# A two-layer graph kernel: fences on TensorE's own queue, a half clip ahead of the logits, gathers behind folds, loads in halves, more logits inside the products

## The chip, the cores and the metric

The kernel runs on one core of one Trainium2 chip. The metric is the device time of one launch in microseconds (us). A core has TensorE (PE in the profile, with its weight loads as PEld), VectorE (DVE), ScalarE (ACT), GpSimd (POOL) and SyncE (SP, which here only issues DMAs and, before the change, empty instructions). Each has its own in-order queue; SP and POOL issue the DMAs, all of which share 16 DMA engines.

## The reference

Eight graphs of 2048 nodes with 256 features share one 0/1 adjacency. Layer 0 is attention in chunks: for every query the softmax is taken in each chunk of 256 keys by itself, and the eight results are added. Layer 1 is graph attention over all keys.

```python
# layer 0 (4 heads of 64, 8 chunks of 256 keys)
h = maximum(layernorm(x), 0); q, k, v = projections of h
scores = clip(q.k / 8, -10, 10);  scores = where(adj == 0, -10, scores)
attn = softmax(scores within each chunk);  ctx = sum over chunks of attn @ v
out = layernorm(ctx @ Wo.T + bo + h) * gamma + beta;  x = x + out
# layer 1
h = maximum(layernorm(x), 0) @ W
e = leaky_relu(h.a1 + (h.a2)^T);  e = where(adj == 0, -1e9, e)
x = x + maximum(softmax(e) @ h, 0)
```

## The kernel before

**Layer 0** is class `Attention`. One batch has 32 steps: 4 blocks of 512 queries times 8 chunks of 256 keys (two key tiles, `kt` 0 and 1). Everything is float32, and one head has 64 rows, so TensorE works on half its rows (64 of 128) and on a quarter of its columns (32) at a time: a "slot" is four such column tiles of 512 queries, in the two passes that float32 takes here. A step has 17 slots, named by two digits in `slots` (L680): eight `o` (logits of heads 0 to 3 and key tile 0 or 1, L555, into the PSUM tile `ps_s`, one tile with both key tiles of a head), eight `v` (values, L570: half 0 or 1 and turn 0 or 1 in the first digit, key tile in the second, into `ps_n`), and one `s` (sums of the exponentials, L592, into `ps_t`). A slot uses the low or the high half of the rows; two neighbours on different halves run side by side, so the order in `begin` (L695) and `end` (L724) is written as pairs. There are two `ps_s`, two `ps_n` and two `ps_t`.

The logits of step `f` pass through DVE (`clip`, L604: the clip and the adjacency in one instruction, both key tiles at once, or in two "half clips" for head 0 of the next step at the end of an even step), ACT (`exponentials`, L616), POOL (`add`, L623, two key tiles added, two instructions a step), a DMA that adds the upper half of the rows to the lower (`fold`, L630, from POOL's queue), TensorE's sums two steps later, ACT (`invert`, L636), DVE (`scale`, L649: `ps_n` times the inverse, into `prod`, two instructions) and a second accumulating DMA (`gather`, L653: `prod` is added to `ctxT` in SBUF; POOL's queue as well). `prod` has two buffers, and all gathers of one block of queries add to one tile, so that each waits for the one before it to land. Before the change `gather(f - 3)` is issued in `end(f)` between the two adds, after whatever `begin(f)` and `end(f)` run "beside" the step on POOL.

The values of turn 0 and turn 1 of one half write the same bank of PSUM from different halves of the rows. `fence` (L522) keeps them apart: an empty instruction on SP waits for the turn-0 matmuls, and the turn-1 matmuls wait for it. SP issues in order all of the kernel's other loads: the adjacency bounds (L179), the transposed features (L163, whose issue waits for the sends of L151), `x` and `h` of a block (L787, L798). `output_tiled` (L811), the output projection, uses the same fence.

**Beside the attention**, class `Between` (L774) does the rest of layer 0 and the start of layer 1 for the block that is ready: its table `beside` (L965) gives a half step (`begin` or `end`) to every piece: loads, features, output projection (L806, L828), layer norms, the value matmuls of layer 1. `adjacency` (L329) does the finds and turns of the adjacency matrix in batch 0, and the table `once` the weights of layer 1 (`layer1_vector`, L1220).

**Layer 1** is `weights` (L1063, DVE, ACT and POOL make the exponentials), `products` (L1083; 64 matmuls of 128x128 by 128x257 for each of 16 pieces, L1090) and `finish` (L1103). The loop over `pieces1` also prepares the projection of the batch after next (`far`), and calls `Attention.early` in its last pieces, which places logits, clips and exponentials of the next batch's first step into the products.

The accumulators of layer 1 are two `ps_s` halves or `ps_n`/`ps_t`; the tile that `add` and `fold` write is the one that layer 1 used as `g`, so that the first add of a batch waits for the last product of the batch before it (releaser "PE ps_t L1090").

Of the kernel before, what the change touches and what calls it, by code (L numbers as in the profile page):

```python
# [17 lines left out]
P = 128  # L18
# [13 lines left out]
def gnn_two_layers(  # L32
# [296 lines left out]
    def adjacency(parts):  # L329
# [14 lines left out]
        finds = [9, 10, 13, 14, 17, 18, 21, 22]  # L344
        turns = [12, 14, 16, 18, 20, 22, 24, 30]
# [176 lines left out]
    def fence(before, after):  # L522

        nop = nc.sync.nop()
        for x in before:
            tc.add_manual_dep(nop.ins, x.ins.name, SYNC, reason="both write one bank of PSUM")
        for x in after:
            tc.add_manual_dep(x.ins, nop.ins.name, SYNC, reason="both write one bank of PSUM")


    class Attention:
# [28 lines left out]
        def values(self, n, half, turn, kt):  # L560
# [4 lines left out]
            if (n, c) not in self.num:  # L565
                self.num[n, c] = ps_n()
            made = []
# [9 lines left out]
            elif kt == 0:  # L577
                fence(self.before.pop((n, c)), made)
# [79 lines left out]
        def early(self, part):  # L658
# [16 lines left out]
            if part == 3:  # L675
                for kt in range(KT):
                    self.logits(1, 0, kt)
                    self.logits(1, 1, kt)

        def slots(self, f, *names):  # L680


            for name in names:
                kind, what, kt = name[0], int(name[1]), int(name[2])
                if kind in "oc":
                    n = f + (what < 2) + (kind == "c")
                    if self.has(n) and (n > 1 or n == 1 and what > 1):
                        self.logits(n, what, kt)
# [6 lines left out]
        def begin(self, f, pieces=()):  # L695
# [10 lines left out]
            if f == 1:  # L706
                self.clip(1, 0)
                self.exponentials(1, 0)
            self.clip(f, 1)
            self.clip(f, 2)  # L710
            self.exponentials(f, 1)
            self.exponentials(f, 2)
            if f == 1:
                self.add(0, 0)
                self.add(0, 1)
                self.fold(0)
            if self.has(f) and odd:
# [6 lines left out]
        def end(self, f, pieces=()):  # L724
# [6 lines left out]
            else:  # L731
                self.slots(f, "v20", "s00", "v21", "o01")
            self.clip(f, 3)
            self.run(pieces, None)
            if odd:
                self.clip(f + 1, 0)
            else:
                self.clip(f + 1, 0, slice(0, 1))
                self.clip(f + 1, 0, slice(1, KT))
# [5 lines left out]
            self.gather(f - 3)  # L745
# [28 lines left out]
    class Between:  # L774
# [7 lines left out]
        def load(self):  # L782
            if self.proj.b == 0:
                self.x4 = load_x(0, self.nb, "x", NNB)
            else:
                self.x4 = xpool.tile([P, TB, F], F32, tag="x", name="x", bufs=NNB)
                nc.sync.dma_start(self.x4, ready_d[self.proj.b % 2]["xb"][self.nb])  # L787

        def features(self):
            self.o4 = work.tile([P, TB, F], F32, tag="o4", name="o4", bufs=1)  # L790
            if self.proj.b == 0:
                for t in range(TB):
# [4 lines left out]
            else:  # L797
                nc.sync.dma_start(self.o4, ready_d[self.proj.b % 2]["hb"][self.nb])  # L798
# [12 lines left out]
        def output_tiled(self, turn):  # L811
# [5 lines left out]
            if turn == 0:  # L817
                self.pp = {t2: ps_t() for t2 in range(2)}
                self.made = {}
            made = {}  # L820
            for i in range(2):
                for c in range(FC):
                    for half in range(2):
                        t2 = half ^ turn
                        rows = slice(half * DH, (half + 1) * DH)
                        for h in range(4):
# [6 lines left out]
                            made.setdefault(t2, []).append(job)  # L833
# [692 lines left out]
```

## Time and profile before

| what | value |
|---|---|
| median of 3 runs | 3804.88 us (3792.54 to 3806.83) |
| profiled execution | 3811.24 us, span 3809.5 us |
| TensorE busy | 3554.2 us, 93% of the span |
| DVE, ACT, POOL busy | 2724.6, 2095.0, 2014.7 us |
| mean granted TensorE clock | 0.975 |
| values, logits, sums (L570, L555, L592) | 1679.1, 1675.6, 270.1 us busy, much of it side by side |
| products (L1090), three groups | 451.4, 293.9, 291.2 us |
| DMA | 512.07 MB, mean 134 GB/s |

Times in the timeline count from the start of the span. "idle 6.42 <-DVE prod L649" means that the engine did nothing for 6.42 us before this instruction, and that the DVE instruction of line 649 on tile `prod` is what released it. "SPq" is SP's sequencer, so the empty instruction of `fence` appears as SPq L524. A busy TensorE is not one at full rate: at a granted clock of one half its instructions take twice as long and still count as busy.

### The profile page before, as it was taken

The page shows a single profiled execution, that of the slowest core. Times are in us where ns is not written, and L with a number is a line of the kernel's source. Part 1 is how long each engine was busy: PE and PEld are TensorE (multiplying, and loading weights), DVE is VectorE, ACT ScalarE, POOL GpSimd, SP SyncE. Part 2 cuts the span into 40 slices and gives each one's busy share as a digit, 9 for nine tenths or more (in the row PEclk, how much of TensorE's full clock was granted, in tenths as well). Part 3 has the DMA queues.
Part 4 walks back from the last instruction along what each step waited for, and adds up shares of the span by engine and source line. Part 5 has one row for each costly group of instructions (what it writes and reads, how often), then busy time and mean ns, then how long its engine had stood idle before and what let it go on. Part 6 is the DMA issues. An engine that isn't in the chain of part 4 may idle for free.

```text
span 3809.5 us, 102046 instructions
## 1 busy us (share of the span) xinstructions
PE 3554.2 (93%) x44032; PEld 1993.3 (52%) x44032; DVE 2724.6 (72%) x3787; ACT 2095.0 (55%) x3689; POOL 2014.7 (53%) x1365
## 2 busy tenths in 40 slices
PE   8888899999999899999999999999999989999889
PEld 4233485434854358443684337743476434854358
DVE  6867487775867758677586776777677776758766
ACT  5677444765356743577436764367643765147651
POOL 2577345873268623677038771377514874048631
PEclk9999999999999999999999999999999999999999
DMA  6767555775457754578436784377733876237751
GB/s 220 172 131 143 121 153 130 153 151 134 136 108 154 143 123 149 113 141 165 109 127 134 140 173 106 113 139 153 169 111 99 160 147 148 75 73 153 147 105 53
DMA packets 234418, 512.07 MB, mean 134 GB/s; under 512 B 44656, under 2 KB 106352, under 8 KB 217584
## 3 DMA queue, kind: packets, MB, share of 16 engines
q0 software_dynamic: 52736, 251.69, 36.9%
q1 hardware_dynamic: 172912, 252.81, 22.4%
q8 instruction: 346, 5.67, 0.6%
q10 hardware_dynamic: 8320, 1.05, 0.2%
q14 instruction: 104, 0.85, 0.1%
HBM read 173.02 MB, written 80.79 MB: 67 GB/s over the span
## 4 chain that ended last, share of the span: by engine, by line
PE 48%; issue 16%; DVE 16%; DMA 10%; ACT 3%; POOL 3%; SPq 1%; DVEq 0%; POOLq 0%; ACTq 0%
PE ps_n L570 16%; PE ps_s L555 15%; DMA ctx<-prod 8%; DVE w L1067 5%; DVE e L604 4%; DVE w L1073 3%; PE ps_s L1090 3%; PE ps_n L1090 3%; PE ps_t L1090 3%; PE ps_t L592 2%; PE ps_t L828 2%; POOL g L623 2%; DVE prod L649 2%; DMA g<-g 1%; ACT hn L382 1%
## 5 line engine op out<-in xcount | busy, mean ns | idle before, releaser
L570 PE MATMUL ps_n<-e,v 64*32 64x512 f32 x16384 | 1679.1, 607 | 150.4 <-DVE prod L649 92.4
L555 PE MATMUL ps_s<-q,k 64*32 64x512 f32 x16384 | 1675.6, 602 | 38.3 <-DVE e L604 29.9
L604 DVE SCALAR_TENSOR_TENSOR e<-ps_s,bound 128x1024 f32<-128x1024 f32 (+1 forms) x1144 | 1247.6, 1108 | 473.2 <-PE ps_s L555 406.0
L623 POOL TENSOR_TENSOR g<-e 128x1024 f32<-128x1024 f32 x512 | 1316.5, 2577 | 368.7 <-PE ps_t L1090 157.3
L616 ACT ACTIVATE e<-e 128x1024 f32<-128x1024 f32 x1024 | 1067.2, 1053 | 656.8 <-DVE e L604 646.8
L570 PEld LDWEIGHTS ps_n<-e,v 64*32 64x32 f32 x16384 | 480.9, 109 | 683.1 <-issue 323.4
L555 PEld LDWEIGHTS ps_s<-q,k 64*32 64x32 f32 x16384 | 477.5, 107 | 631.0 <-issue 383.7
L649 DVE TENSOR_TENSOR prod<-ps_n,rz 128x512 f32<-128x512 f32 x448 | 290.7, 683 | 267.7 <-PE ps_n L570 190.3
L1090 PE MATMUL ps_s<-g,w 128*128 128x257 f32 x2048 | 451.4, 382 | 5.0 <-DVE w L1073 5.0
L1090 PEld LDWEIGHTS ps_s<-g,w 128*128 128x128 f32 x2048 | 391.5, 191 | 62.2 <-DVE w L1073 6.1
L1073 DVE SCALAR_TENSOR_TENSOR w<-bound,w 128x1024 f32<-128x1024 int8 x256 | 345.7, 1350 | 8.7
L1067 DVE TENSOR_SCALAR w<-src,cd 128x512 f32<-128x512 f32 x512 | 327.0, 680 | 7.0 <-ACT src L1048 6.6
L1113 POOL TENSOR_TENSOR x<-x,r 128x256 f32<-128x256 f32 x124 | 93.1, 797 | 390.7 <-ACT r L1111 390.7
L1090 PE MATMUL ps_n<-g,w 128*128 128x257 f32 x1024 | 293.9, 384 | 0.0
L1090 PE MATMUL ps_t<-g,w 128*128 128x257 f32 x1024 | 291.2, 381 | 0.0
L436 POOL TENSOR_TENSOR krn<-krn 128x4 f32<-128x4 f32 x28 | 11.6, 413 | 518.5 <-ACT krn L435 518.5
L653 POOL DMA_DIRECT2D ctx<-prod x224 | 205.4, 917 | 140.7 <-DMA ctx<-prod 88.9
L592 PE MATMUL ps_t<-g,ones 64*32 64x512 f32 x2048 | 270.1, 592 | 8.6 <-DMA g<-g 8.1
L630 POOL DMA_DIRECT2D g<-g x256 | 212.6, 831 | 77.2 <-POOL g L623 65.7
L636 ACT ACTIVATE rz<-ps_t 128x512 f32<-128x512 f32 x256 | 152.1, 594 | 144.1 <-PE ps_t L592 131.2
L1090 PEld LDWEIGHTS ps_n<-g,w 128*128 128x128 f32 x1024 | 194.1, 191 | 44.9 <-issue 18.4
L1090 PEld LDWEIGHTS ps_t<-g,w 128*128 128x128 f32 x1024 | 194.9, 190 | 28.4
(155 smaller groups left out, 3102.3 us busy)
## 6 DMA issues: line engine op xcount, KB each, us to landing
g<-g POOLq DMA_DIRECT2D x256, 512.0 KB, 6.1
ctx<-prod POOLq DMA_DIRECT2D x224, 512.0 KB, 5.5
bound<-bound_d SPq DMA_DIRECT2D x256, 256.0 KB, 4.0
turned_d<-squares SPq DMA_DIRECT2D x232, 128.0 KB, 2.8
hT<-turned_d SPq DMA_DIRECT2D x58, 512.0 KB, 4.6
rows<-in_adj_dram SPq DMA_DIRECT2D x32, 512.0 KB, 5.8
out_dram<-x SPq DMA_DIRECT2D x31, 512.0 KB, 2.9
hb_d<-hn SPq DMA_DIRECT2D x56, 256.0 KB, 3.5
```

The lines of the kernel that those rows point to most:

```text
L555: nc.tensor.matmul(self.s[n, o][c * Q:(c + 1) * Q, kt, :], self.k[p][rows, at:at + Q], self.q[p][rows, nb * NB:(nb + 1) * NB], start=True, ...
L570: made.append(nc.tensor.matmul(self.num[n, c][h * Q:(h + 1) * Q, :], self.v[rows, j * KT + kt, at:at + Q], self.e[n, h // 2][rows, h % 2 * ...
L592: nc.tensor.matmul(self.total[n][h * Q:(h + 1) * Q, :], ones[rows, :], self.both(n)[rows, h, :], start=True, stop=True,)
L604: nc.vector.scalar_tensor_tensor(self.e[n, p][:, i * KT:(i + 1) * KT, :][:, kts, :], self.s[n, o][:, kts, :], -CLIP * SC, bounds[nb, j // ...
L616: nc.scalar.activation(e, e, AF.Exp, scale=1.0 / SC)
L623: nc.gpsimd.tensor_tensor(self.both(n)[:, 2 * p:2 * p + 2, :][:, heads, :], e[:, 0, heads], e[:, 1, heads], op=ALU.add)
L630: nc.gpsimd.dma_start(self.both(n)[mine], self.both(n)[other], accum_op=ALU.add)
L649: nc.vector.tensor_tensor(dst[:, c, :], self.num.pop((n, c)), self.rz[n], op=ALU.mult)
L653: nc.gpsimd.dma_start(self.ctxT[self.STEPS[n][0]], self.prod.pop(n), accum_op=ALU.add)
L1067: nc.vector.tensor_scalar(w[:, i, :], self.src[nb], self.cd[:, 0, j:j + 1], self.cd[:, 1, j:j + 1], op0=ALU.mult, op1=ALU.max,)
L1073: nc.vector.scalar_tensor_tensor(two, bounds[nb, j4][:, i - 1:i + 1, :], 0.0, two, op0=ALU.is_gt, op1=ALU.mult)
L1090: nc.tensor.matmul(accs[t][:, 0:F + 1], w[:, i, t * P:(t + 1) * P], g[0][:, j, :], start=j == 0, stop=j == NT - 1,)
```

## The change

Six things change.

1. `fence` makes its empty instruction on TensorE's queue, and takes only what has to be over; the matmuls behind it are in the same queue. The fence of `output_tiled` stands before all of turn 1.
2. At the end of an even step the slots `v21` and `o01` are written after the first half clip. Both key tiles of a head's logits are parts of one `ps_s` tile.
3. `gather(f - 3)` is issued in `begin(f)`, on POOL's queue right behind `fold(f - 1)`, before the pieces beside.
4. The loads of `x` and `h` of a block become two DMAs each, and the features of a block are set two half steps earlier; those of a batch's last block go behind the attention (`ready_last`), with one addition (`mid.add(1)`), which thereby moves from POOL to DVE.
5. A fourth part of `early` clips heads 0 and 1 of step 1 and makes the logits of its heads 2 and 3, between the two halves of the last product (and at the end of the setup); what `begin(1)` did of this is left out there.
6. In batch 0 the adjacency's finds are spread over even half steps, the vectors of layer 1 are multiplied late and in four pieces, and the first bounds are fetched earlier in the setup. In layer 1's loop, the loads, sends and norms of the next projections come up to one product earlier.

```diff
-    def fence(before, after):
-        nop = nc.sync.nop()
+    def fence(before):
+        nop = nc.tensor.nop()
         for x in before:
             tc.add_manual_dep(nop.ins, x.ins.name, SYNC, reason="both write one bank of PSUM")
-        for x in after:
-            tc.add_manual_dep(x.ins, nop.ins.name, SYNC, reason="both write one bank of PSUM")
...
         def values(self, n, half, turn, kt):
+            if turn and kt == 0:
+                fence(self.before.pop((n, c)))
...
-            elif kt == 0:
-                fence(self.before.pop((n, c)), made)
...
         def early(self, part):
...
+            else:
+                for o in range(2):
+                    self.clip(1, o)
+                    self.exponentials(1, o)
+                for kt in range(KT):
+                    self.logits(1, 2, kt)
+                    self.logits(1, 3, kt)
...
         def begin(self, f, pieces=()):
...
-            if f == 1:
-                self.clip(1, 0)
-                self.exponentials(1, 0)
-            self.clip(f, 1)
+            if f > 1:
+                self.clip(f, 1)
             self.clip(f, 2)
...
+            self.gather(f - 3)
...
         def end(self, f, pieces=()):
...
-                self.slots(f, "v20", "s00", "v21", "o01")
+                self.slots(f, "v20", "s00")
             self.clip(f, 3)
             self.run(pieces, None)
-            if odd:
+            if odd or not self.has(f):
                 self.clip(f + 1, 0)
             else:
                 self.clip(f + 1, 0, slice(0, 1))
+                self.slots(f, "v21", "o01")
                 self.clip(f + 1, 0, slice(1, KT))
...
             self.add(f, 0)
-            self.gather(f - 3)
             self.add(f, 1)
             self.fold(f)
...
     class Between:
-        def load(self):
+        def load(self, t2):
...
+                two = slice(2 * t2, 2 * t2 + 2)
+                nc.sync.dma_start(self.x4[:, two, :], ready_d[self.proj.b % 2]["xb"][self.nb][:, two, :])
...
-                -3: [self.load],
-                8: [self.features, lambda: self.bias(0)],
+                -3: [lambda: self.load(0)],
+                -1: [lambda: self.load(1)],
+                6: [late(lambda: self.features(0))],
+                8: [late(lambda: self.features(1)), late(lambda: self.bias(0))],
...
-        finds = [9, 10, 13, 14, 17, 18, 21, 22]
-        turns = [12, 14, 16, 18, 20, 22, 24, 30]
+        finds = [6, 10, 14, 18, 22, 30, 34, 38]
+        turns = [8, 12, 16, 20, 24, 32, 36, 40]
...
+        if nb == 2:
+            for part in range(3):
+                fetch_bounds(0, part)
...
-    for part in range(3):
-        fetch_bounds(0, part)
     att.early(0)
...
     att.early(3)
+    att.early(4)
...
-        6: [lambda: layer1_vector(0)],
-        7: [lambda: layer1_vector(1)],
+        43: [lambda: load_vector(0), lambda: load_vector(1)],
+        46: [lambda: layer1_vector(0, 0)],
+        50: [lambda: layer1_vector(0, 1)],
+        62: [lambda: layer1_vector(1, 0)],
+        65: [lambda: layer1_vector(1, 1)],
...
-            one.products(accs[nb], ws.pop(i), j4)
+            if ahead and i == len(pieces1) - 1:
+                one.products(accs[nb], ws[i], j4, range(2))
+                att.early(4)
+                one.products(accs[nb], ws.pop(i), j4, range(2, TB))
+            else:
+                one.products(accs[nb], ws.pop(i), j4)
```

## The prediction

> **What bounds the kernel now.** I read the page's busy table and groups first, then the waits, then the timeline of a plain stretch of attention and of each long wait of TensorE. TensorE is busy 93% of the span, so the question is what its idle 250 us are, and whether the change makes new ones. The waits name them (engine, line, releaser; us in total, times, longest):
>
> ```profile
> PEld ps_n L570 <- SPq L524: 102.1, 237, 9.3
> ...
> PE ps_n L570 <- DVE prod L649: 92.4, 93, 7.0
> POOL ctx L653 <- DMA ctx<-prod: 88.9, 22, 9.1
> ...
> DVE prod L649 <- DMA ctx<-prod: 55.7, 15, 7.5
> ...
> PE ps_n L570 <- SPq L524: 39.0, 11, 8.4
> ```
>
> SP's fence costs TensorE itself only 39.0 us, in 11 places; the 102.1 are weight loads that come early anyway. The largest item, 92.4 us behind `prod`, is two things: about 0.45 us in every plain pair of steps, and seven long ones. The end of a plain even step (batch 2) on TensorE, then on DVE:
>
> ```profile
> 1124.27 0.64 PE L570 MATMUL ps_n<-e,v 64*32 64x512 f32 x4
> 1124.39 0.61 PE L592 MATMUL ps_t<-g,ones 64*32 64x512 f32 x4
> ...
> 1125.13 0.64 PE L570 MATMUL ps_n<-e,v 64*32 64x512 f32 x4
> 1125.25 0.61 PE L555 MATMUL ps_s<-q,k 64*32 64x512 f32 x4
> ...
> 1128.46 0.63 PE L570 MATMUL ps_n<-e,v 64*32 64x512 f32 x4 [0.45 <-DVE prod L649]
> ```
>
> ```profile
> 1124.53 1.23 DVE L604 SCALAR_TENSOR_TENSOR e<-ps_s,bound 128x1024 f32<-128x1024 f32 x1 [1.08 <-PE ps_s L555]
> 1126.43 1.29 DVE L604 SCALAR_TENSOR_TENSOR e<-ps_s,bound 128x512 f32<-128x512 f32 x2 [0.67 <-PE ps_s L555]
> 1127.63 1.28 DVE L649 TENSOR_TENSOR prod<-ps_n,rz 128x512 f32<-128x512 f32 x2
> ```
>
> A slot is two passes 0.43 apart, 0.86 us; `v20` runs beside `s00` (1124.27, 1124.39), `v21` beside `o01` (1125.13, 1125.25), then `o10` beside `v30` and `o11` beside `v31`. DVE ends the clip of step f at 1125.76, waits 0.67 for `o01`, does both half clips and the scales, and `v00` of the next step starts at 1128.46, 4.19 after `v20`. Two such steps take 15.36 us (from the starts of successive sums: 7.85 and 7.51).
>
> The long wait of batch 1, on POOL, DVE and TensorE:
>
> ```profile
> 776.84 0.82 POOL L630 DMA_DIRECT2D g<-g  x1 [0.29 <-POOL g L623]
> 787.39 0.19 POOL L370 TENSOR_TENSOR rn<-rn,mv 128x4 f32<-128x4 f32 x1 [9.73 <-ACT rn L366]
> ...
> 789.94 0.82 POOL L653 DMA_DIRECT2D ctx<-prod  x1
> ```
>
> ```profile
> 799.88 1.29 DVE L649 TENSOR_TENSOR prod<-ps_n,rz 128x512 f32<-128x512 f32 x2 [6.88 <-DMA ctx<-prod]
> ```
>
> ```profile
> 800.63 1.08 PE L570 MATMUL ps_n<-e,v 64*32 64x512 f32 x4 [6.42 <-DVE prod L649]
> ```
>
> POOL stands 9.73 us at a tiny instruction of the layer norm with `add` and `gather` queued behind it; the gather is issued at 789.94, lands 9.8 us later, and until then the second `prod` buffer isn't free.
>
> SP's wait of the same batch, and the granted clock around it (third number from the right; the first is the length of the stretch, the second TensorE's busy time):
>
> ```profile
> 893.46 3.69 PE L570 MATMUL ps_n<-e,v 64*32 64x512 f32 x32 [2.92 <-SPq L524]
> ```
>
> ```profile
> 885.00:892.50 7.50, 5.54 (x47) 1.70 (x45) 4.25 (x3) 3.51 (x6) 4.39 (x4) 1.00 1.01 212
> 892.50:899.40 6.90, 5.94 (x35) 1.92 (x36) 1.29 (x2) 0.00 (x0) 2.19 (x2) 0.51 1.02 254
> ```
>
> The fence is queued in SP behind a load of transposed features (L163, issued 891.83), and after 2.92 idle us the clock is 0.51 for 6.9 us: the same 32 matmuls take 3.69 where 1.95 is the row just before.
>
> **The change, part by part**, against the profiled execution (3811.24 us, 6.4 above the median).
>
> *Fences.* SP's 39.0 us go: 15.5 in batch 0 (1.18, 3.36, 2.66, 8.35) and 23.5 in batches 1 to 7 (2.92 to 4.14). The values then wait for turn 0 in their own queue; that is at least one pair of slots (0.86 us) earlier, and TensorE's nop has nothing else to wait for. Late next is nothing that these values use; 2 us may remain. Gain 37. `output_tiled` waits for a gather (L806 <- DMA ctx) 3.20, 3.06 and 3.11 us, and L828 9.4 us in 14 pieces; both gathers now go out before the pieces beside. Gain 6 and 6 (bounds 0 and 18.8).
>
> *Gather behind fold.* Idle at step 20 of batches 1 to 7 is 6.42, 7.01, 5.02, 6.39, 4.29, 5.57 and 6.12, 40.8 in all. The gather leaves before POOL's layer norm piece, so its landing no longer holds `prod`. Late next is the fold of step 20, issued behind the same piece: the sums two steps later need it. I put 1.2 each, from the 0.8 to 1.3 that its 6.1 us landing leaves over; 32.4 gained. At step 28 seven waits of 1.05 to 1.12 are of the same kind: 4.5 of 7.4. Two of batch 0 (2.50, 4.85): 5 of 7.35. TensorE's waits for folds at L592, 8.3 us: 3. On POOL all adds of a step come 0.92 later behind the gather's issue, inside a slack that I count under the rivals.
>
> *Batch 0 and setup.* The first clip waits 6.6 us for its bounds, TensorE 5.33; fetched two blocks earlier, they are there: 5. `layer1_vector` sits on DVE ahead of a half clip and costs 4.73 at 106.96: 4.7.
>
> Together 103.6.
>
> *Clock.* A mean of 0.975 over 3809.5 us is at most 190 us at one half, 95 us lost. After the stalls at step 20 the steps are 15.66 long in the mean, 2.15 more than a plain step (7.68) and the idle time (5.83): 15 for seven. After SP's waits TensorE is the bound (3.4 of 6.9 us lost): 24 for seven. Batch 0 has five such windows, up to 17. Ends 0 and 56, if other gaps throttle instead; I take 36, since the stalls in front of most of them go. The Trainium skill, "TensorE: Matmul & The Clock Gate", section "What's actually happening", has the clock fall after at least one idle window of some 3.4 us. The row above shows half clock after 2.92. By the rule, the four SP waits of 2.92 to 3.21 would cost no clock, 14 of the 36 us would not come back, and the sum would be 14 higher.
>
> *Half clip ahead of `o01`.* Here the change adds a wait. Half clip 0 can start at the end of clip(f,3), without its 0.67. But `o01` writes the other half of the tile that half clip 0 reads, and a write to the tile is held behind an earlier read of it. `o01` now waits for that half clip, and TensorE's queue stands behind it. With P the start of `v20`: `v21` runs alone to P+1.71; clip(f,3) ends at P+1.49, half clip 0 (0.69) at P+2.18; `o01` starts at P+2.28 instead of P+0.98, beside `o10`; then `v30` with `o11`, then `v31` alone to P+4.85. DVE's chain (`o01` 0.86 and some 0.3 to its release, half clip 1 0.69, scale 0.68, 0.15) ends at P+4.9 as well. So `v00` moves from P+4.19 to P+4.9: 0.71 us more per plain pair. There are 120 such places (15 a batch). In two per batch, where DVE's wait was 0.42, it costs 1.0; where DVE had no wait (a dozen, mostly batch 0), up to 1.5. Going through all 120 gives 99: 86 in batches 1 to 7 and 12.7 in batch 0, of which I take 10, as DVE is late there for other reasons. Loss 96. Bounds: 0, if the wait didn't exist, and 120 at 1.0 each.
>
> *Logits in the products.* Four slots more, half clips and exponentials go into the last product: 1.95 us on TensorE, gone later from step 1. But POOL's first add waits for the last product to leave the tile (157.3 us in 7 waits), and the first sums for its fold: the sums' slack was 0.1, 0.4, 0.5, 2.0, 2.1, 0.4 and 0.7. A gap of 1.29 at the head of each batch goes. Net +1 each, +7 (bounds -9 and +14).
>
> *Loads in halves, later features, pieces in layer 1's loop, vectors:* 56 more SP issues on a queue that blocks nobody now: 0, covered by loads that are early by a step or more; uncovered, 56 times the 0.42 that an issue of a bound (L179) takes on SP, 24.
>
> Sum: 3811.2 - 103.6 - 36 + 96 + 7 = 3774.6; by the median 3768, rounded to 3770.
>
> **Rivals.**
>
> A. *The stalls move on rather than go.* For: the layer norm still stops POOL 9.7 us, with the fold behind it; idle time elsewhere was masked by the stall. Half of the 139.6 gained, 70, against 103 lost: 3844, by the median 3838. Against: the landing that ended the wait was the gather's. Intermediate cases, three quarters of the gain, give about 3805, no change.
>
> B. *The chain of gathers becomes the bound* (slower). Each waits for the one before to land, and now its data stand behind the fold's.
>
> ```profile
> g<-g POOLq DMA_DIRECT2D x256, 512.0 KB, 6.1
> ctx<-prod POOLq DMA_DIRECT2D x224, 512.0 KB, 5.5
> ```
>
> POOL's work per step is 2 x 2.58 + 0.83 + 0.92 = 6.9 of 7.68 us. The queue's 251.69 MB took 36.9% of the span, 5.6 us for a fold with a gather, so I estimate 7.2 to 7.5 from issue to landing, under the new step of 8.04. Beyond 8.04 every microsecond counts 224 times. Excess of 0.16 on all eats the forecast's gain; 0.4 gives 3770 + 90 = 3860. For: a gather beside other loads took 9.8. Against: in the plain stretch DMA engines have gaps.
>
> C. *The wait at `o01` is covered.* Then 96 is not lost: 3672. For: 0.45 of idle is there at `v00`. Against: the chain above loses on TensorE and DVE alike.
>
> **How the numbers follow.** Forecast (3740 to 3790) 0.45; A with its intermediate cases 0.25 (3790 to 3840); B 0.18 (3815 to 3900); C, or a loss of half its size, 0.12 (3670 to 3740). The range leaves out the far half of B and of C: 3700 to 3850. Half a per cent, 19 us, is about what a measurement of this kernel can tell from no change: faster (below 3786) is the forecast nearly whole, C and a little of A: 0.59; same 0.14; slower 0.27.
>
> **What the profile after would show.** No SPq releaser at L570; a plain pair of 16.0 to 16.1 us with an idle 0.5 to 0.6 in front of `o01`, released by DVE e, 120 times; step 20 below 10 us and POOL's gather ahead of the layer norm; a clock near 0.985. Wrong would be a pair of 15.4 (C), gathers waiting for landings in plain steps (B), and step 20 still near 14 with fold as its releaser (A).

## The result, and the profile after

The changed kernel takes 3909.54 us (median of 4 runs), the kernel before 3805.36: a ratio of 1.029 with a 95% interval of 1.026 to 1.032, 104 us slower. The forecast was 35 us faster. Of two versions further down one execution each was far slower than the rest (5184 and 9321 us); their ratios leave it out, and without it their medians are 0.7 and 2.6 us lower.

The profiled execution has a span of 3906.7 us, 97 more than before (3809.5). TensorE's busy time grew from 3554.2 to 3645.1 us for the same number of instructions, and its share stayed at 93%, so most of the loss does not show as idle time: two slots side by side count their time once, a slot that runs alone has it for itself. The granted clock is 0.979, where it was 0.975. The waits after (engine, line, releaser; us in total, times, longest):

```profile
POOL g L621 <- PE ps_t L590: 166.2, 110, 6.0
...
PE ps_s L553 <- DVE e L602: 107.7, 228, 5.6
POOL ctx L651 <- DMA ctx<-prod: 99.0, 32, 9.6
...
PEld ps_n L570 <- DVE prod L647: 49.1, 93, 2.3
...
PE ps_s L553 <- ACT r L1123: 36.7, 7, 14.6
```

No wait names SPq any more, and the 92.4 us of values behind `prod` are gone from the list. In their place, logits wait for DVE's clips (29.9 us in 37 places before, 107.7 in 228 now), and in seven places for the end of layer 1, 36.7 us.

To see where the 97 us lie, the two executions are cut at the same instructions: the first and last sums of a batch (L592 and L590), its first and fourteenth group of products (L1090 and L1102, each group 32 matmul instructions in the trace, which are 16 matmuls in two passes and not 64 matmuls), and the end of its last product. Added over eight batches, in us:

| stretch | before | after | difference |
|---|---|---|---|
| start to the first sums | 103.4 | 95.1 | -8.3 |
| first to last sums of each batch | 2203.5 | 2235.4 | +31.9 |
| last sums to the first product | 440.4 | 474.2 | +33.8 |
| first to fourteenth group of products | 762.3 | 802.3 | +40.0 |
| from there to the last product | 209.0 | 219.3 | +10.3 |
| to the next batch's first sums, or the end | 90.9 | 80.3 | -10.6 |

So a third of the loss is in the attention, where some steps got longer, others shorter, and each of the two by more than that; the rest lies outside it, in stretches for which the prediction had small terms. First the attention: the end of a plain even step (batch 2), TensorE and then DVE.

```profile
1141.52 0.64 PE L570 MATMUL ps_n<-e,v 64*32 64x512 f32 x4
...
1142.38 1.06 PE L570 MATMUL ps_n<-e,v 64*32 64x512 f32 x8
1143.66 1.09 PE L553 MATMUL ps_s<-q,k 64*32 64x512 f32 x16 [0.22 <-DVE e L602]
...
1148.48 0.63 PE L553 MATMUL ps_s<-q,k 64*32 64x512 f32 x4 [0.30 <-DVE e L602]
```

```profile
1144.79 0.69 DVE L602 SCALAR_TENSOR_TENSOR e<-ps_s,bound 128x512 f32<-128x512 f32 x1 [1.19 <-PE ps_s L553]
1145.40 0.68 DVE L647 TENSOR_TENSOR prod<-ps_n,rz 128x512 f32<-128x512 f32 x1
1146.51 0.69 DVE L647 TENSOR_TENSOR prod<-ps_n,rz 128x512 f32<-128x512 f32 x1 [0.43 <-PE ps_n L570]
1147.12 2.45 DVE L602 SCALAR_TENSOR_TENSOR e<-ps_s,bound 128x1024 f32<-128x1024 f32 x2
```

`v21` runs alone from 1142.38, and `o01` starts at 1143.66, released by DVE, 2.14 behind `v20` (the prediction had 2.28). But the pair of steps takes 16.40 us (8.55 and 7.85), not 16.07. The predicted chain stopped one link early: `v31`, now alone and late, is what the second scale waits for (0.43 at 1146.51), the clip behind that scale starts at 1147.12, and the logits that need the PSUM tile which that clip frees wait at 1148.48, 6.96 behind `v20`, where the same logits (`o30`) came at about 5.9 before.

In layer 1 the early logits of the next batch, which need the PSUM tiles of block 2's accumulators, now wait for its end (batch 1):

```profile
1063.83 1.06 PE L553 MATMUL ps_s<-q,k 64*32 64x512 f32 x8 [4.04 <-ACT r L1123]
```

```profile
1060.82 1.23 DVE L1085 SCALAR_TENSOR_TENSOR w<-bound,w 128x1024 f32<-128x1024 int8 x1
1061.96 0.15 DVE L1120 TENSOR_SCALAR rz<-ps_s 128x1 f32<-128x1 f32 x1
```

DVE stands 9.1 us behind TensorE here (block 2's last product ends at 1052.86). Before, it stood 4.2 us behind (that product ended at 1045.14), and the logits had no wait there:

```profile
1049.34 0.15 DVE L1108 TENSOR_SCALAR rz<-ps_s 128x1 f32<-128x1 f32 x1
```

And the output projection of the last block waits for a gather:

```profile
919.10 3.75 PE L816 MATMUL ps_t<-woT,ctx 128*128 128x256 f32 x8 [3.76 <-DMA ctx<-prod]
```

The same eight matmuls took 1.96 us before, behind a shorter wait for something else:

```profile
914.35 1.96 PE L806 MATMUL ps_t<-woT,ctx 128*128 128x256 f32 x8 [0.83 <-DVE v L515]
```

At 3.75 they run at about half clock behind the gap: from 919.0 to 925.6 the granted clock is 0.54.

### The profile page after: what moved, and what is told of

Same layout as the page of the kernel before. It is cut to its first block, busy times and chain, and to the rows that moved or that the text cites. A ratio compares the mean times of both kernels' runs of the same rounds, so it can differ in the third digit from the quotient of the medians.

```text
span 3906.7 us, 101545 instructions
## 1 busy us (share of the span) xinstructions
PE 3645.1 (93%) x44032; PEld 1990.0 (51%) x44032; DVE 2727.3 (70%) x3795; ACT 2091.3 (54%) x3689; POOL 2023.5 (52%) x1357
## 3 DMA queue, kind: packets, MB, share of 16 engines
q0 software_dynamic: 52736, 251.69, 36.7%
q10 hardware_dynamic: 8320, 1.05, 0.2%
## 4 chain that ended last, share of the span: by engine, by line
PE 53%; DVE 22%; DMA 9%; issue 6%; POOL 5%; ACT 4%; SPq 0%; ACTq 0%; DVEq 0%; POOLq 0%
PE ps_s L553 16%; PE ps_n L570 13%; DVE e L602 8%; DVE w L1079 5%; DMA ctx<-prod 5%; POOL g L621 3%; PE ps_n L1102 3%; DVE w L1085 3%; PE ps_t L1102 3%; PE ps_s L1102 3%; PE ps_t L839 2%; PE ps_t L590 2%; DMA prod<-in_x_dram 2%; DVE prod L647 2%; PE ps_n L496 2%
## 5 line engine op out<-in xcount | busy, mean ns | idle before, releaser
L553 PE MATMUL ps_s<-q,k 64*32 64x512 f32 x16384 | 1617.7, 603 | 144.9 <-DVE e L602 107.7
L621 POOL TENSOR_TENSOR g<-e 128x1024 f32<-128x1024 f32 x512 | 1264.9, 2543 | 416.7 <-PE ps_t L1102 220.6
L553 PEld LDWEIGHTS ps_s<-q,k 64*32 64x32 f32 x16384 | 441.4, 107 | 712.0 <-DVE e L602 261.8
L1102 PE MATMUL ps_s<-g,w 128*128 128x257 f32 x2048 | 447.6, 380 | 0.0
L1102 PEld LDWEIGHTS ps_s<-g,w 128*128 128x128 f32 x2048 | 388.8, 190 | 56.1
L1085 DVE SCALAR_TENSOR_TENSOR w<-bound,w 128x1024 f32<-128x1024 int8 x256 | 344.4, 1345 | 8.7
L1079 DVE TENSOR_SCALAR w<-src,cd 128x512 f32<-128x512 f32 x512 | 338.7, 703 | 7.0 <-ACT src L1060 6.6
L651 POOL DMA_DIRECT2D ctx<-prod x224 | 228.9, 1022 | 215.3 <-DMA ctx<-prod 99.0
L1102 PE MATMUL ps_n<-g,w 128*128 128x257 f32 x1024 | 298.9, 389 | 3.9 <-DVE w L1085 3.9
L590 PE MATMUL ps_t<-g,ones 64*32 64x512 f32 x2048 | 271.2, 593 | 26.6 <-DMA g<-g 23.5
L1102 PE MATMUL ps_t<-g,w 128*128 128x257 f32 x1024 | 293.4, 383 | 0.0
L1102 PEld LDWEIGHTS ps_n<-g,w 128*128 128x128 f32 x1024 | 195.2, 193 | 59.3 <-issue 27.8
L1102 PEld LDWEIGHTS ps_t<-g,w 128*128 128x128 f32 x1024 | 196.8, 192 | 29.7
```

The source lines that it names most:

```text
L553: nc.tensor.matmul(self.s[n, o][c * Q:(c + 1) * Q, kt, :], self.k[p][rows, at:at + Q], self.q[p][rows, nb * NB:(nb + 1) * NB], start=True, ...
L590: nc.tensor.matmul(self.total[n][h * Q:(h + 1) * Q, :], ones[rows, :], self.both(n)[rows, h, :], start=True, stop=True,)
L621: nc.gpsimd.tensor_tensor(self.both(n)[:, 2 * p:2 * p + 2, :][:, heads, :], e[:, 0, heads], e[:, 1, heads], op=ALU.add)
L651: nc.gpsimd.dma_start(self.ctxT[self.STEPS[n][0]], self.prod.pop(n), accum_op=ALU.add)
L1079: nc.vector.tensor_scalar(w[:, i, :], self.src[nb], self.cd[:, 0, j:j + 1], self.cd[:, 1, j:j + 1], op0=ALU.mult, op1=ALU.max,)
L1085: nc.vector.scalar_tensor_tensor(two, bounds[nb, j4][:, i - 1:i + 1, :], 0.0, two, op0=ALU.is_gt, op1=ALU.mult)
```

## The experiments: what the changed kernel lost

Four versions of the changed kernel, with parts undone. The first puts `o01` beside `v21` again:

```diff
-                self.slots(f, "v20", "s00")
+                self.slots(f, "v20", "s00", "v21", "o01")
             ...
                 self.clip(f + 1, 0, slice(0, 1))
-                self.slots(f, "v21", "o01")
                 self.clip(f + 1, 0, slice(1, KT))
```

> The changed kernel with one part undone: at the end of an even step o01 is issued beside v21 again, ahead of the first half clip. Theory H (the wait of o01 for the first half clip is the main loss): a plain pair falls from 16.40 to 15.36 us, 120 places give back 100 to 125 us, about 3795 us. Rival R (the loss comes from folds and gathers that land later, and the longer pairs hide it): pairs get shorter, but steps wait for landings instead, and less than 60 us come back, over 3850 us.

Measured 3847.97 us, ratio to before 1.0114 (1.0086 to 1.0142): 62 us of the loss are back. Plain pairs fell to 15.36 as Theory H had it, and still only about half of its 100 to 125 us came, just above what R allowed (under 60): other steps got longer. The sums now wait for folds, which the longer pairs had hidden:

```profile
PE ps_t L590 <- DMA g<-g: 69.8, 37, 6.7
```

In the changed kernel that wait is 23.5 us, in the kernel before 8.1. So H names the largest single part, and R is right that it hid something.

The second puts the loads, sends, norms and flips of layer 1's loop back where they were.

```diff
-            if far and i in (2, 5, 8, 11):
-                far.send(k)
-                far.ready(k)
+            if far and i in (3, 6, 9, 12):
+                far.send(i // 3 - 1)
+                far.ready(i // 3 - 1)
...
-            if far and i in (1, 4, 7, 10):
+            if far and i in (2, 5, 8, 11):
                 for t2 in range(2):
-                    far.norm(k, t2)
+                    far.norm(i // 3, t2)
```

> The changed kernel with one part undone: in layer 1's loop, loads, sends, norms and flips of the next projections are placed as before. Theory L (they put DVE behind with the weights of the products, so that the finish of block 2 and the early logits behind it come late): the products of batches 0 to 5 are 6 to 7 us shorter from the first product to the fourteenth, TensorE's wait for ACT r of 4 to 5 us (14.6 in batch 0) goes, 35 to 50 us in all, about 3868 us. Rival E (the early logits in the last product are what the longer products come from): within 8 us of the changed kernel.

Measured 3867.79, ratio 1.0159 (1.0133 to 1.0186): 42 us back, Theory L's number. The stretch from first to fourteenth products falls from 802.3 to 758.5 us. Batch 6, which has no projection to prepare, had 92.2 in every version. In the changed kernel the instructions that make the weights take longer, in the group of the changed kernel and then of this one:

```profile
L1079 DVE TENSOR_SCALAR w<-src,cd 128x512 f32<-128x512 f32 x512 | 338.7, 703 | 7.0 <-ACT src L1060 6.6
```

```profile
L1079 DVE TENSOR_SCALAR w<-src,cd 128x512 f32<-128x512 f32 x512 | 327.0, 681 | 7.0 <-ACT src L1060 6.6
```

Same work, 22 ns more each in the mean. In batch 1, from the first product to block 2's end, DVE was busy 4.7 us longer (83.6 for 78.9) with the same 115 instructions, and idle as long as before; the instructions that make the weights (L1079, L1085) account for all of it. What changed beside them is POOL: 16 of its large TENSOR_TENSOR instructions for the next projection (L444, L445) stand in this stretch, where 12 did. The two traces show what that does. Of the 512 instructions of L1079, none that ran with no TENSOR_TENSOR of POOL beside it took over 548 ns, in either version; those that lay wholly beside such work took 1193 ns in the mean with the loop undone and 1219 in the changed kernel. Wholly or in part beside it ran 124 with the loop undone, 136 in the changed kernel.

The third has both of these edits.

> Both parts undone. If the two losses lie in different stages and add: 140 to 170 us off the changed kernel, about 3755 us, below the kernel before by some 50. If the gains of the fences and the gathers were never there (rival R): 3790 to 3815, no better than before.

Both undone gives 3810.39, ratio 1.0014 (0.9998 to 1.003). Against the changed kernel 99 us, where the two alone add to 103: they do add, in different stages. But the version is no faster than the kernel before, as R had it: of the predicted gains nothing is to be seen.

The next leaves out the fourth part of `early` too:

```diff
-            if ahead and i == len(pieces1) - 1:
-                one.products(accs[nb], ws[i], j4, range(2))
-                att.early(4)
-                one.products(accs[nb], ws.pop(i), j4, range(2, TB))
-            else:
-                one.products(accs[nb], ws.pop(i), j4)
+            one.products(accs[nb], ws.pop(i), j4)
...
+            if f == 1:
+                self.clip(1, 0)
+                self.exponentials(1, 0)
```

> Both parts undone, and the fourth part of early as well (its clips, exponentials and logits are in step 1 again). If the logits inside the last product cost what the trace shows (the last product 2.0 us longer, the head of the next batch 0.5 shorter): some 10 us below the version with both parts undone. If step 1 takes back what the product gives up: within 4 us of it.

3799.01, ratio 0.9978 (0.9959 to 0.9997): 11 us, the size that was expected, with intervals that nearly touch. In the two traces the last products take 207.8 us for 220.6, and 5.8 are given back at the head of the next batch, 7 us in all; the attention is another 9.5 shorter, which the expectation doesn't explain.

## The experiments: where the gains went

From here on the question is why the fences and the gather, which were to bring 100 us and more, brought nothing. Each part alone, on the kernel before; first the fences (the diff shown in the change).

> The kernel before with the fences alone changed. Prediction: 37 us of SP's waits and some 28 us of half clock behind them go, 40 to 65 us faster, about 3750. Rival (the end of a batch's attention is bound by the last gathers and the load of the transposed features, which land no earlier): TensorE waits there instead, the stretch from the last sums to the first product grows by as much as the last step shrinks; within 15 us of the kernel before.

3800.56 us, ratio 0.9987 (0.9971 to 1.0002), 6 us and not clear of the noise: the rival. TensorE has no SPq wait, and the attention is 41.3 us shorter; the stretch from the last sums to the first product is 35.6 us longer. In batches 1 to 6 the output projection of the last block starts 280.4 us in the mean after the first sums with the old fence and 280.5 with the new: it waits for the last gather, which lands when it did.

```profile
876.01 0.89 POOL L651 DMA_DIRECT2D ctx<-prod  x1 [4.32 <-DMA ctx<-prod]
...
885.09 0.87 POOL L651 DMA_DIRECT2D ctx<-prod  x1 [6.90 <-DMA ctx<-prod]
890.16 0.88 POOL L651 DMA_DIRECT2D ctx<-prod  x1 [4.20 <-DVE stats L358]
```

```profile
896.86 3.75 PE L804 MATMUL ps_t<-woT,ctx 128*128 128x256 f32 x8 [3.41 <-DMA ctx<-prod]
```

These are batch 1's last three gathers. The first two wait for the landing of the one before; the third is issued 0.5 us behind the landing of the second (889.62) and put down by the profile to a DVE instruction of the same time. Also unforeseen: the stall at step 20 shrinks with the fences alone (the three steps' sum around it from 31.1 to 27.1 us in batch 1). Before, that gather was issued at 789.94 and a load of x at 790.09, and it took 9.8 us; here no load stands beside it, and it takes 5.7.

On top of the fences, the half clip's new place:

```diff
-                self.slots(f, "v20", "s00", "v21", "o01")
+                self.slots(f, "v20", "s00")
...
                 self.clip(f + 1, 0, slice(0, 1))
+                self.slots(f, "v21", "o01")
                 self.clip(f + 1, 0, slice(1, KT))
```

> The kernel before with the fences and the half clip changed: against the version with the fences alone, the half clip's own cost. Theory H: 1.04 us in every plain pair, 105 to 125 us slower than that version. The prediction's size: 0.71 in a plain pair, 90 to 100. Rival (the longer pairs leave landings more time, and waits behind folds and gathers go with them): 50 to 80, as the changed kernel's own undoing of it gave 62.

3884.46, ratio 1.021 (1.018 to 1.024), 84 us above the fences alone: between the sizes that were written down. Plain pairs are at 16.40 again (1.04 each), and the waits for folds fall from 31.2 to 5.6 us, which is part of the difference to 120 times 1.04.

The gather's new place on the kernel before, with the fences on SP:

```diff
         def begin(self, f, pieces=()):
...
+            self.gather(f - 3)
...
         def end(self, f, pieces=()):
...
             self.add(f, 0)
-            self.gather(f - 3)
             self.add(f, 1)
```

> The kernel before with the gather's new place alone. Prediction: the seven stalls of some 6 us at step 20 shrink to 1.2, 30 to 45 us faster, about 3770. Theory G (the stall is the landing of that one gather beside a load of x, and the gather in front of both adds makes folds wait elsewhere): stalls at step 20 shrink, but waits at the sums grow by 20 to 50 us, the kernel is 0 to 20 us slower than before.

Measured: 3777.49, ratio 0.9918 (0.9895 to 0.994), 28 us faster, just short of the 30 to 45 expected. Steps 20 and 21 take 8.7 and 8.4 us where they had taken 15.7 and 7.6 in the mean of batches 1 to 7; the waits for folds are 12.4 us. SP's waits grow from 39.0 to 56.9 us; that TensorE now arrives earlier would explain it, but isn't shown.

Then two versions of the one with three parts undone (3799 us). One has the loads, the features and `ready_last` as before:

```diff
-                -3: [lambda: self.load(0)],
-                -1: [lambda: self.load(1)],
-                6: [late(lambda: self.features(0))],
-                8: [late(lambda: self.features(1)), late(lambda: self.bias(0))],
+                -3: [self.load],
+                8: [self.features, lambda: self.bias(0)],
```

> The version with the half clip, layer 1's loop and the early logits undone (3799 us), with the loads undone as well: whole loads of x and h, features at the old half step, those of the last block inside the attention, the addition on POOL. Theory D (features and x of two blocks are issued in one burst around step 25, the fold beside them lands late, and the sums wait 2 to 5 us for it; the last block's features behind the attention slow the last gather): the waits at the sums fall from 62 to below 25 us, steps 26 and 27 together from 26 to 20 us in batches 1 to 7, 30 to 50 us in all, about 3760. Rival G (the gather in front of both adds holds POOL, and so the folds, whatever is loaded): within 12 us of 3799.

3798.31, ratio 0.9986 (0.9968 to 1.0003), no difference: Theory D falls as far as the halves and the half steps go. The waits at the sums stay at 54.3 us. Whether its burst of loads is to blame is another question, since whole loads behind the new fences can go out in a burst too.

The other has the gather in its old place:

```diff
         def begin(self, f, pieces=()):
...
-            self.gather(f - 3)
...
         def end(self, f, pieces=()):
...
             self.add(f, 0)
+            self.gather(f - 3)
             self.add(f, 1)
```

> The version with the half clip, layer 1's loop and the early logits undone (3799 us), with the gather between the two adds again. Theory P (the prediction's: the gather ahead of the layer norm piece removes the stall at step 20): the seven stalls of some 6 us return, 30 to 40 us slower, about 3835. Theory G (the gather ahead of the adds makes each fold wait for the landing of the gather before; POOL waits 150 us for landings): the waits at the sums fall from 62 to below 30 us, which pays for the stalls; within 12 us of 3799, or faster.

3784.06, ratio 0.994 (0.9916 to 0.9965): 15 us faster with the gather in its *old* place, with the waits at the sums at 24.0, as Theory G had both. So the place that gains 28 us with the old fences costs 15 with the new.

Both parts, fences and gather, on the kernel before:

> The kernel before with the fences and the gather's new place. Alone they gave 6 and 28 us. If they add (prediction's way of summing): 34 us faster, about 3772. Theory C (the end of a batch is bound by its last gathers, whatever comes before): no more than the gather alone, 3775 to 3785. Theory G (with the fences gone SP's loads run into the folds, and the gather ahead of both adds holds POOL at a late landing): 3785 to 3800, and the waits at the sums are above 40 us, where the gather alone had 12.5.

3815.65, ratio 1.0022 (1.0007 to 1.0036): the two parts alone clash. The waits at the sums are 50.1 us:

```profile
PE ps_t L590 <- DMA g<-g: 50.1, 24, 6.0
```

SP's queue in batch 2, first with the gather alone, then with the fences too:

```profile
1281.33 0.34 SPq L798 DMA_DIRECT2D o<-hb_d  x1
1282.01 0.46 SPq L179 DMA_DIRECT2D bound<-bound_d  x1
1294.76 0.32 SPq L787 DMA_DIRECT2D x<-xb_d  x1
```

```profile
1274.74 0.34 SPq L796 DMA_DIRECT2D o<-hb_d  x1
1275.12 1.03 SPq L179 DMA_DIRECT2D bound<-bound_d  x1
1276.20 0.49 SPq L785 DMA_DIRECT2D x<-xb_d  x1
1276.78 0.47 SPq L179 DMA_DIRECT2D bound<-bound_d  x1
1277.35 0.54 SPq L163 DMA_DIRECT2D hT<-turned_d  x1
```

The old fence's empty instructions stood between these loads, and each held SP until TensorE had come so far. Without them 2 MB go out within 2.6 us. A fold issued by POOL at 1279.68 then lands 10.1 us later, and TensorE's sums start at 1289.95:

```profile
1279.68 0.83 POOL L628 DMA_DIRECT2D g<-g  x1 [0.29 <-POOL g L621]
...
1289.95 1.08 PE L590 MATMUL ps_t<-g,ones 64*32 64x512 f32 x4 [4.01 <-DMA g<-g]
```

To test that, the spacing alone is put back: beside each fence an empty instruction on SP, for which nothing waits.

```diff
         nop = nc.tensor.nop()
         for x in before:
             tc.add_manual_dep(nop.ins, x.ins.name, SYNC, reason="both write one bank of PSUM")
+        pace = nc.sync.nop()
+        for x in before:
+            tc.add_manual_dep(pace.ins, x.ins.name, SYNC, reason="spaces the loads behind it")
```

> Fences on TensorE and the gather's new place (3816 us), and beside every fence an empty instruction on SP that waits for the same turn-0 values; nothing waits for it. Theory S (the old fence also spaced SP's loads: without it x, bounds, h and the transposed features of a block go out within 3 us, and a fold beside them takes 10 us instead of 6): the waits at the sums fall from 50 to below 20 us, and the kernel is at least as fast as the gather alone (3777), 3745 to 3778. Rival C (the fences and the gather clash at the last gathers only): the waits at the sums stay above 35 us, 3800 to 3815.

3766.82, ratio 0.9902 (0.9871 to 0.9933): 49 us faster than without the spacing, with nothing else changed, and the waits at the sums are 16.4 us:

```profile
PE ps_t L593 <- DMA g<-g: 16.4, 21, 3.3
```

Theory S is shown, for the gather in its new place. SP's loads of this place are now apart, and the three folds among them take 5.4 to 6.5 us to land:

```profile
1270.92 0.34 SPq L799 DMA_DIRECT2D o<-hb_d  x1
1271.31 0.89 SPq L179 DMA_DIRECT2D bound<-bound_d  x1
1283.76 0.32 SPq L788 DMA_DIRECT2D x<-xb_d  x1
1290.62 0.32 SPq L179 DMA_DIRECT2D bound<-bound_d  x1
1291.03 1.23 SPq L163 DMA_DIRECT2D hT<-turned_d  x1
```

Against the gather alone (3777) the intervals overlap, and the fences with the spacing but without the gather's move were not run. So what the new fences are worth once the loads are spaced is not shown.

## The experiments: the end of a batch, and the fastest version

That the last gathers bound the end of a batch is tested by making the last two of them on DVE, which is idle there:

```diff
         def gather(self, n):
-            if n in self.prod:
+            if n in self.prod and n >= len(self.STEPS) - 2:
+                ctxT = self.ctxT[self.STEPS[n][0]]
+                nc.vector.tensor_tensor(ctxT, ctxT, self.prod.pop(n), op=ALU.add)
+            elif n in self.prod:
                 nc.gpsimd.dma_start(...)
```

> The kernel before with the fences changed, and the last two gathers of a batch (steps 30 and 31) made by DVE additions in place of DMAs. Theory C (the end of a batch's attention is bound by the chain of its last gathers, which end the output projection's wait 281 us after the first sums with either fence): the output projection starts at 9.8 to 10.5 us behind the last sums instead of 15.4, and 40 to 55 us come off the version with the fences alone, about 3752. Rival F (the transposed features bound it, or the projection's own inputs): within 12 us of that version.

3764.74, ratio 0.9887 (0.9867 to 0.9906), 36 us faster than the fences alone and a little under the expected 40. In the two traces 25 us lie between the last sums and the first product, where the fences had added 36; the rest is spread over the other stretches. The additions take 1.22 us each, where a gather takes 5.4 to land, and the projection has no gather to wait for:

```profile
883.80 1.22 DVE L652 TENSOR_TENSOR ctx<-ctx,prod 128x1024 f32<-128x1024 f32 x1 [8.24 <-DMA ctx<-prod]
...
886.25 1.22 DVE L652 TENSOR_TENSOR ctx<-ctx,prod 128x1024 f32<-128x1024 f32 x1
```

The projection starts 12.8 us behind the last sums in the mean of batches 1 to 6, from 15.3; the 9.8 expected isn't reached, as layer 1's value matmuls now wait for `prod` in that place (1.99 us in batch 1).

The same additions in the version with half clip, loop, early logits and gather undone (3784 us):

> The same for the version with half clip, layer 1's loop, early logits and gather undone (3784 us), which keeps the fences, loads and batch 0's pieces. Theory C: 40 to 55 us off, about 3737, the fastest so far. Rival F: within 12 us of 3784.

3761.77, ratio 0.9869 (0.9836 to 0.9902): 22 us off, less than Theory C's 40. In the traces the stretch behind the last sums is 39 us shorter, and the attention 11 longer.

And with the loads undone as well:

> The same again with the loads undone too, so that of the change only the fences and batch 0's pieces stay. If the loads in halves and the later features of the last block are worth nothing (as with the gather in its new place): within 6 us of the version that keeps them. If the features behind the attention did slow the last gathers: the two are equal now that no gather is left there, and the load burst at step 25 decides, 5 to 20 us in favour of the old loads.

3772.44, ratio 0.9908 (0.9886 to 0.9929): the loads in halves are worth 8 to 11 us here if anything, as the intervals overlap.

The additions with fences and the gather's new place, and then in the changed kernel without its three losing parts:

> The same with the last two gathers of a batch as DVE additions. Theory C: the gather's gain shows now, about 25 us below the version with fences and these additions (3765), 3740. Theory G: no faster than that version, 3760 to 3780, with waits at the sums above 40 us.

3811.06, ratio 1.0006 (0.9988 to 1.0025): no gain, waits at the sums 60.6 us. So the end of a batch was not what hid the gather's gain in this company.

> The changed kernel with half clip, layer 1's loop and early logits undone (3799 us) and the last two gathers as DVE additions. Theory C: 35 to 50 us off, about 3757. Theory G (waits at the sums of 62 us stay): 15 to 35 us off, 3765 to 3785, so that the gather's old place (3762) is not beaten.

3788.1, ratio 0.9961 (0.9946 to 0.9976): 11 us, below the range of either theory; the gather's old place isn't beaten.

Last, additions and spacing together, in the same two versions:

> The same with the last two gathers of a batch as DVE additions (3811 us without the spacing). Theory S: with spaced loads and no gather at the end both gains show, 3725 to 3755, the fastest so far. Rival C: 3790 to 3811.

3764.08, ratio 0.9885 (0.9842 to 0.9928): not below the spaced version without the additions (3766.82), and no part of 3725 to 3755. The waits at the sums are 19.1 us, so it isn't the folds that took the gain. In the two traces the stretch behind the last sums is 18 us shorter with the additions, and 13 us of that are lost again before the first sums and in the attention; why is open.

> The changed kernel with half clip, layer 1's loop and early logits undone, the last two gathers as DVE additions (3788 us), and the spacing on SP. Theory S: 20 to 45 us off, 3743 to 3768; what remains against the version above is the worth of the loads in halves and of batch 0's pieces, which I expect to be 5 to 15 us slower or faster. Rival C: within 10 us of 3788.

3736.56, ratio 0.9821 (0.978 to 0.9861): 52 us faster than the same version without the spacing, more than the 20 to 45 expected, 28 below the version above where 5 to 15 were expected, and the fastest of all: 70 us below the kernel before, 173 below the changed one. It keeps of the change the fences, the gather's place, the loads in halves, and batch 0's pieces; it leaves out the half clip's place, layer 1's loop and the fourth part of `early`, and adds the spacing on SP and the two additions on DVE.

## Why the prediction was wrong

It summed to 37 us faster and came out 104 slower. With the half clip, the loop and the early logits undone the changed kernel takes 3799 us, 8 below the kernel before, where gains of 140 us were forecast (103.6, and 36 of clock): 132 us of gains did not come. The loop cost 42 us for 0, the early logits 4 more than forecast, the half clip 34 less. That makes 144 of the difference of 141. By steps:

- *Fences, 37 us, 12 more at the output projection, and their share of 36 us of half clock.* Wrong, and the larger error. The waits went as said, but alone the fences gave 6 us, which the noise covers. "Late next is nothing that these values use" looked only at the values; late next was the output projection, behind three gathers in a chain. And SP's loads were costed as "a queue that blocks nobody now", 0 to 24 us of issue time: the blocked queue had spaced the loads, and with the gather in its new place the burst cost 49 and 52 us, as the spacing showed when it was put back.
- *Gather behind fold, 45 us in its terms.* Right in direction for the kernel before, where it gave 28 us alone, and wrong in company with the new fences, where it cost 15. The stall at step 20 did go in the changed kernel (8.2 us in the mean of batches 1 to 7, for 15.7); the waits at the sums grew instead, from 8.1 to 23.5 us, and to 61.8 with the half clip, the loop and the early logits undone. Rival B had the place (landings, POOL held) but not the cause. Its 7.2 to 7.5 us from issue to landing came out at 7.6 in the median (5.5 before), though its own figures give 5.9 and not 5.6 us for a fold with a gather, which are 1.05 MB.
- *Half clip, 96 us lost.* The mechanism was right: `o01` waits for the half clip in 111 of the 120 places, 0.22 us in a plain one where 0.5 to 0.6 was forecast. The size per plain pair was short, 1.04 for 0.71, since the chain was followed to `v00` and not through the second scale to the next clip. In the sum it was too large, 84 alone and 62 in the changed kernel, in part because longer pairs hide late folds (25 us of waits at the sums, of the 41 that 84 falls short of 120 times 1.04).
- *Layer 1's loop, 0 us.* Wrong: 42 lost. "Covered by loads that are early" looked at transfers; what moved was POOL work that runs beside DVE's weights and makes them longer, and DVE was already 4 us behind TensorE at the point where the early logits wait.
- *Logits in the products, 7 us lost.* Right in direction and about in size, 11. But the gap at the head of a batch, which was to go, did not: 1.29 us before, 2.05 now in seven places, released by the end of layer 1 (ACT r).
- *Setup and batch 0, 10 us.* Start to first sums is 8 us shorter, where 5 of the 10 lay; the other 5, of `layer1_vector`, were not measured by themselves.
- *Clock.* Of the 96 us that half clock cost (0.975 of 3809.5 us) 15 came back and not 36 (0.979 of 3906.7). The term counted long stalls, and the traces show half clock behind short gaps too, shorter than the 2.92 us of the row in the prediction and than the rule weighed there asks for. In the kernel before, batch 2 starts so: between 1080 and 1091 the row below has the only gap of over 0.3 us, and from 1087.1 to 1090.5 the granted clock is 0.50.

```profile
1084.64 1.92 PE L555 MATMUL ps_s<-q,k 64*32 64x512 f32 x16 [1.29 <-DVE rz L1108]
```

Of the rivals, A (the stalls move on) describes the fences; none reached the measured time, since each was priced with all other terms as forecast. The slowest, B, worked out at 3860 and had a range up to 3900.

## What to carry to other kernels

When a wait is removed, ask for two things that are not in its row: who arrives next at the same end of the stage (here a chain of three gathers, which put the end of the attention at 280 us with either fence), and what the wait had held back (here loads, which it had kept 7 to 13 us apart). A queue that is blocked by a dependency also paces what is behind it; if transfers in bursts hurt, put the spacing back without the wait. When work is moved to another engine's idle time, ask which instructions it will then run beside. And a chain that is added to a pipeline is to be followed until it meets an engine that was idle, not to the first instruction that waited before.

## What was not expected of the hardware

A fold of 512 KB, 5.8 us from issue to landing in the median, took 10 us beside 2 MB of loads issued within 2.6 us, and a gather with a load of x issued 0.15 us behind it took 9.8; the mean rate over the span, 134 GB/s, gives no hint of this. The same DVE instruction (128x512, float32) took 540 ns in the mean with no TENSOR_TENSOR of POOL beside it and 1219 ns wholly beside such work; moving POOL's work by one product took its mean from 681 to 703 ns, 12 us over 512 instructions. And accumulating into SBUF by DVE took 1.22 us for a tile whose accumulating DMA needs 5.2 to 7.9 in the medians of these runs.
